# Attention layers of a sparse graph network: queries as two float32r numbers, spread over slots by two products each; slot numbers and owners in 16 bits

## The chip, the core and the metric

The kernel runs on one core of a Trainium2 chip, in one launch. The metric is the device time of that core in microseconds (us). Five engines take part, each with its own queue in program order: TensorE (PE) multiplies matrices into PSUM, VectorE (DVE) and ScalarE (ACT) work element by element, GpSimd (POOL) does some of that and also issues the indirect gathers, and SyncE (SP) issues most other transfers.

## The reference, cut to what matters

Four layers run in a row on x of shape 8 x 2048 x 128, with one sparse 0/1 matrix `adj` (2048 x 2048, symmetric, with its diagonal; about 17 ones in a row). Layers 0 and 2 are masked multi-head attention with a feed-forward part, layers 1 and 3 are graph attention with scores that are sums of two numbers per node.

```
# layers 0 and 2 (8 heads of 16)
Q, K, V = h @ Wq, h @ Wk, h @ Wv
scores  = where(adj == 0, -inf, Q K^T / 4)           # per batch and head
x = layer_norm(h + softmax(scores) V @ Wo + bo)
x = layer_norm(x + relu(x @ W1 + b1) @ W2 + b2)
# layers 1 and 3
h = x @ W;  e = leaky_relu(h @ a_src (of i) + h @ a_dst (of j)), masked by adj
x = layer_norm(softmax(e) h + x)
```

## The kernel before, in words

**Units, steps, slots.** The 2048 nodes are cut into 32 units of 64 nodes (`UNIT`), and the 8 batches into two halves, so that 128 partitions hold 64 nodes of two batch halves. For each unit the kernel lists at run time the neighbours that its nodes need. The list has nine tiles of 128 slots; a slot belongs to one owner node and names one source node. A unit is worked in five steps (`TG`): four of two tiles and a last one of one tile. A dense fallback stands behind a count of rows that don't fit; it is not entered here.

**One step of an attention layer** (`attention`). POOL issues one indirect gather per tile (`gather`, L1671): 128 rows of 8 KB, keys and values of all batches, into one of six `kv` buffers. PE spreads the unit's queries over the step's slots (`spread`, L1734): a 0/1 matrix `hot` (which node owns which slot) times the queries `q_sb`, one product of 32 rows by 512 columns for each tile and batch half, so four of them in a two-tile step, in four different groups of 32 rows of the array; the one-tile step has two of 64 rows. The result `qe` fills four of the eight PSUM banks, and there is one buffer of it. DVE multiplies the gathered keys by `qe` (`multiply`, L1746) and sums over the 16 numbers of a head (`reduce`, L1753). ACT takes the exponential (L1763). POOL, in some steps DVE, multiplies the values by it (`weigh`, L1773; where DVE does it, ACT first writes the exponentials to a PSUM buffer, `ps_e`). PE adds up the slots of each owner with the second half of `hot` (`add`, L1805) into `acc` and `sums`.

**Opening a unit** (`opened`, `fetch`). SP loads the unit's x (L1371, one of four buffers) and its `hot` as 8-bit numbers (L1386); ACT widens `hot` to float32 (L1393, one of three buffers); PE makes the queries in four products of 128 columns (`queries`, L1826, into a PSUM buffer `ps_q`), and ACT copies them out (L1830) into `q_sb`, of which there are two buffers.

**After the last step** (`after_attention`). Division (L1870), transpose (L1482), Wo (L1505), addition (L1882), centring (L1495), norm (L1607, L1640), feed-forward (L1505, L1902, L1912), second norm, store of the new x (L1359), and the projection for the next layer's table (L1535 or L1533, stored at L1593). All these products, the queries, and `ps_e`, share the two PSUM buffers of the pool "m".

**The order.** Nothing is written out in place. Each piece is recorded as an operation with a cost per engine, a key and the cells it reads and writes; a list scheduler (`Plan.order`) walks through assumed time, gives each free engine its ready operation with the lowest key, counts buffers, and so fixes the order on every engine. The engines then run that order with semaphores. The spread has the key of its step minus 6, `queries` and the copy the key of the unit minus 4, most of `after_attention` the key of the unit plus 5. A cost that changes in the code can therefore move any instruction in all queues.

**Graph layers** have the same units and slots. ACT rebuilds the first part of `hot` from the slot numbers (`slot`, L1399) and DVE the second from the owners (`owner`, through `slots`, L1317).

Of the kernel before, what the change touches and what calls it, by code (L numbers as in the profile page):

```python
# [9 lines left out]
F32 = mybir.dt.float32  # L10
# [10 lines left out]
P = 128  # L21
# [747 lines left out]
class Sparse:  # L769
# [15 lines left out]
    def __init__(self, ctx, tc, x, xt, xk, adj, w, out):  # L785
        self.tc, self.nc, self.w, self.xt_in, self.xk_in, self.out = tc, tc.nc, w, xt, xk, out
        self.B, self.N, _ = x.shape
        self.NB = self.N // P
        self.NU = self.N // UNIT
        self.HB = self.B // 2  # L790

        def pool(name, **kw):
            return ctx.enter_context(tc.tile_pool(name=name, **kw))

        self.nc.scalar.preload_act_table_set("natural_log_exp_and_others")
        self.const = pool("const", bufs=1)
        self.dram = pool("dram", bufs=1, space=DRAM)
        self.plan = Plan(self.nc)
        self.op, self.cell = self.plan.op, self.plan.cell
        for tag, bufs in SBUF_BUFS.items():  # L800
            self.plan.pool(tag, pool(f"sb_{tag}", bufs=bufs), bufs, tag in BY_KEY)
        for tag, bufs in PSUM_BUFS.items():
            self.plan.pool(tag, pool(f"ps_{tag}", bufs=bufs, space=PSUM), bufs)

        self.constants()
        self.weights_at = [Cell() for _ in LAYERS]
        self.keys_at = Cell()
        self.late = self.tight = False
        self.whole()
        self.gates = {}  # L810

        self.gate = self.keys_at
        keys = self.const.tile([P, 2 * P], F32, name="Wkv_0")
        self.fill(0, (keys[:, 0:P], w[0]["Wk"]), (keys[:, P : 2 * P], w[0]["Wv"]), at=self.keys_at)
        self.layers = [{"Wkv": keys}]


        self.tables = [
            self.dram.tile([self.N, self.B * (2 * P if kind is MHA else P + 2)], F32, name=f"table_{n}")
            for n, kind in enumerate(LAYERS)  # L820
        ]
        self.table = [Cell() for _ in LAYERS]
        self.rest = [Cell() for _ in LAYERS]

        self.xd = self.dram.tile([self.NU, P, CH], F32, name="xd")
        self.x_at = [Cell() for _ in range(self.NU)]
        self.hots = self.dram.tile([self.NU, P, HOT], F8, name="hots")
        self.hots_at = [Cell() for _ in range(self.NU)]
        self.kept = {}
        self.ends_at = [None] * self.NU  # L830
        self.t = self.const.tile([P, self.NU, P // GROUP * self.HB], F32, name="t")
        self.t_at = [Cell() for _ in range(self.NU)]
        self.idx = self.const.tile([P, self.NU, TILES], I32, name="idx")
        self.idx_at = [Cell() for _ in range(self.NU)]


        self.owner = self.const.tile([P, self.NU, TG, 2], F32, name="owner")
        self.ends = self.const.tile([P, self.NU, 2], F32, name="ends")
        self.late_ends = self.const.tile([P, LATE, 2], F32, name="late_ends")
        self.shift = self.const.tile([P, LATE, 2], F16, name="shift")  # L840

        self.empty = self.const.tile([P, self.NU, TILES], F32, name="empty")


        self.seen = self.const.tile([P, 4, self.NB], F32, name="seen")
        self.stats = self.const.tile([P, 6], F32, name="stats")
        self.eps = self.fixed("eps", EPS)
        self.half = self.fixed("half", 0.5)
        self.rows_n = self.fixed("rows_n", float(self.N))
        self.huge = self.fixed("huge", 1e30)  # L850
# [3 lines left out]
    def constants(self):  # L854
# [5 lines left out]
        self.neg_half = const.tile([P, 4], F32, name="neg_half")  # L860
        nc.gpsimd.memset(self.neg_half, -0.5)

        def ramp(name, shape, pattern, base=0, step=0):
            t = const.tile(shape, F32, name=name)
            nc.gpsimd.iota(
                t, pattern=pattern, base=base, channel_multiplier=step, allow_small_or_imprecise_dtypes=True
            )
            return t


        self.slot = ramp("slot", [P, GS], [[1, GS]])
        for g in range(1, P // GROUP, 2):
            nc.gpsimd.iota(
                self.slot[g * GROUP : (g + 1) * GROUP, GS - P : GS],
# [21 lines left out]
            allow_small_or_imprecise_dtypes=True,  # L896
        )

        self.centre = const.tile([P, P], F32, name="centre")
        nc.vector.tensor_scalar(self.centre, self.ident, -1.0 / P, None, ALU.add)  # L900

# [464 lines left out]
    def fetch(self, n, u, key):  # L1366
# [7 lines left out]
            writes=[x],  # L1374
            dma=P * CH * 4,
        )
        hot = self.cell("hot", [P, HOT])
        if n == 0 and u < KEPT:
            hot8 = self.kept[u]
            self.op({"ACT": 1.05}, lambda e: e.copy(hot.tile, hot8.tile), key - 15, reads=[hot8], writes=[hot])  # L1380
# [312 lines left out]
    def attention(self, n):  # L1693
# [4 lines left out]
        for u, t in self.sequence(0):  # L1698
# [29 lines left out]
            def spread(e, t=t, qe=qe, q=q, hot=hot, tiles=tiles):  # L1728
                for j in range(tiles):
                    for hf in range(2):  # L1730
                        at = (2 * hf + j) * GROUP

                        rows = slice(at, at + GROUP * (3 - tiles))
                        e.matmul(  # L1734
                            qe.tile[:, j, hf, :],
                            lhsT=hot.tile[rows, t * P : (t + 1) * P],
                            rhs=q.tile[rows, :],
                            start=True,
                            stop=True,
                        )  # L1740

            op({"PE": 1.2}, spread, key - 6, reads=[q, hot, *self.sources(n, u, t)], writes=[qe])

            def multiply(e, kv=kv, qe=qe, part=part, tiles=tiles):
                k = part(kv, 0)
# [50 lines left out]
            def add(e, t=t, kv=kv, hot=hot, acc=acc, sums=sums, part=part, exps=exps, tiles=tiles):  # L1796
                weights = exps(kv).rearrange("p (q c) -> p q c", q=2 * tiles)
                for out, rhs in ((acc.tile, part(kv, 1)), (sums.tile, weights)):

                    for j in range(tiles):  # L1800
                        for hf in range(2):
                            at = (2 * hf + j) * GROUP
                            rows = slice(at, at + GROUP * (3 - tiles))
                            col = GS + (2 * t + j) * GROUP
                            e.matmul(  # L1805
                                out[rows, :],
                                lhsT=hot.tile[:, col : col + GROUP * (3 - tiles)],
                                rhs=rhs[:, 2 * j + hf, :],
                                start=(t == 0),
                                stop=(t == TG - 1),  # L1810
                            )
# [5 lines left out]
    def opened(self, n, u, base):  # L1817
# [5 lines left out]
        def queries(e, ps=ps, x=x):  # L1823
            for b in range(hb):
                cols = slice(b * P, (b + 1) * P)
                e.matmul(ps.tile[:, cols], lhsT=x.tile[:, cols], rhs=L["Wq"], start=True, stop=True)  # L1826

        q = cell("q_sb", [P, CH])
        op({"PE": 1.1}, queries, base - 4, reads=[x, self.weights_at[n]], writes=[ps], holds=[q])
        op({"ACT": 0.6}, lambda e, q=q, ps=ps: e.copy(q.tile, ps.tile), base - 4, reads=[ps], writes=[q])  # L1830
        acc = cell("acc", [P, CH])
        sums = cell("sums", [P, hb * H])
        return x, hot, q, acc, sums
# [396 lines left out]
```

## Time and profile before

| | |
|---|---|
| median of 6 runs | 2934.63 us (2930.02 to 2937.98) |
| the profiled execution's own time | 2936.81 us |
| its span in the profile | 2935.0 us |
| mean granted TensorE clock | 0.894 |
| DMA | 1022.52 MB, mean 348 GB/s |
| the list of neighbours and layer 0 | about 0 to 1165 us |
| layer 1 | about 1165 to 1580 us |
| layer 2 | about 1580 to 2500 us |
| layer 3 | about 2490 to 2935 us |

The layers run into each other, so the limits are rough. The profile gives for each engine its busy time and what ended its idle time. A product in float32 is recorded as two pairs of weight load and matmul, so that the four products of a two-tile spread are eight records. Matmul ends are modelled, so a busy PE is not PE at its peak. "Granted clock" is the share of its full speed at which TensorE was clocked.

### The profile page before, as it was taken

What the parts mean: (1) busy time and instruction counts of PE and PEld (TensorE: products, weight loads), DVE (VectorE), ACT (ScalarE), POOL (GpSimd) and SP (SyncE); (2) the same over time, 40 slices, a digit from 0 to 9 for tenths busy, and PEclk for the clock granted to TensorE, in tenths of its full rate; (3) what the DMA queues carried; (4) which work ended last, traced back from release to release, by engine and by line L of the source; (5) the groups of instructions that cost most, each with busy time, mean ns of one, the idle gap of its engine ahead of it and who ended that gap; (6) DMA issues with size and microseconds to landing.
All of it is one profiled execution on the core that took longest, in us unless ns stands there. A gap on an engine that the chain in (4) does not pass through costs nothing.

```text
span 2935.0 us, 59465 instructions
## 1 busy us (share of the span) xinstructions
PE 2277.4 (78%) x21668; PEld 1328.7 (45%) x21668; DVE 2302.2 (78%) x3783; ACT 1419.2 (48%) x4899; POOL 2132.7 (73%) x1456
## 2 busy tenths in 40 slices
PE   6567777778788886888886788888878878777775
PEld 4423333333333434676664343334434333566664
DVE  7789989999889994555554888898898898576665
ACT  5536555555544442655553244444444444354443
POOL 1288877888788855666663877888788786677774
PEclk8779989999899997988987789999999999888887
DMA  8788888899899967999997899999998996999996
GB/s 306 283 323 344 328 324 324 339 353 360 322 345 357 367 262 300 380 405 411 405 407 294 331 353 341 374 364 347 358 383 332 351 380 257 343 409 407 408 395 265
DMA packets 248061, 1022.52 MB, mean 348 GB/s; under 512 B 39184, under 2 KB 52880, under 8 KB 175856
## 3 DMA queue, kind: packets, MB, share of 16 engines
q0 software_dynamic: 166464, 864.44, 75.7%
q1 hardware_dynamic: 81296, 154.18, 14.2%
q8 instruction: 174, 2.85, 0.4%
q14 instruction: 127, 1.04, 0.1%
HBM read 978.23 MB, written 88.08 MB: 363 GB/s over the span
## 4 chain that ended last, share of the span: by engine, by line
DMA 26%; PE 20%; DVE 17%; issue 10%; POOL 7%; ACT 3%; SPq 0%; POOLq 0%; DVEq 0%; ACTq 0%
DMA kv<-table,idx 24%; DVE kv L1746 8%; PE qe L1734 5%; POOL kv L1671 4%; DVE s L1753 4%; POOL kv L1773 3%; PE acc L1805 3%; PE ps_c L1495 2%; DMA hot<-hots 2%; DVE kv L1773 2%; PE ps_y L1912 1%; PE acc_q L2009 1%; PE ps_f L1505 1%; PE ps_t L1482 1%; PE ps_o L1505 1%
## 5 line engine op out<-in xcount | busy, mean ns | idle before, releaser
L1671 POOL DMA_INDIRECT kv<-table,idx x1152 | 1198.2, 1040 | 589.6 <-issue 319.4
L1773 POOL TENSOR_TENSOR kv<-kv 128x2048 f32<-128x2048 f32 x260 | 921.3, 3555 | 72.0 <-ACT kv L1763 67.6
L1746 DVE TENSOR_TENSOR kv<-qe,kv 128x2048 f32<-128x2048 f32 (+1 forms) x320 | 662.1, 2069 | 106.7 <-DMA kv<-table,idx 69.2
L1753 DVE TENSOR_REDUCE s<-kv 128x128 f32<-128x2048 f32 (+1 forms) x320 | 659.6, 2061 | 9.0 <-DVE kv L1746 0.5
L1734 PE MATMUL qe<-q_sb,hot 32*128 32x512 f32 (+1 forms) x2304 | 399.1, 695 | 165.4 <-DVE kv L1746 162.9
L1805 PE MATMUL acc<-kv,hot 128*32 128x512 f32 (+1 forms) x2304 | 369.8, 653 | 56.9 <-POOL kv L1773 26.5
L2009 PE MATMUL acc_q<-kv,w 128*32 128x129 f32 (+1 forms) x4608 | 204.5, 311 | 117.7 <-DVE w L1993 97.4
L1993 DVE TENSOR_TENSOR w<-hot,e 128x512 f32<-128x512 f32 (+1 forms) x384 | 221.3, 597 | 49.4 <-ACT e L1983 34.9
L1763 ACT ACTIVATE kv<-s 128x128 f32<-128x128 f32 (+1 forms) x320 | 95.6, 299 | 319.8 <-DVE s L1753 203.3
L1734 PEld LDWEIGHTS qe<-q_sb,hot 32*128 32x128 f32 (+1 forms) x2304 | 106.9, 196 | 296.3 <-DVE kv L1746 243.0
L2009 PEld LDWEIGHTS acc_q<-kv,w 128*32 128x32 f32 (+1 forms) x4608 | 159.2, 127 | 149.2 <-DVE w L1993 111.1
L1971 DVE TENSOR_TENSOR e<-te,kv 128x16 f32<-128x16 f32 (+1 forms) x320 | 58.5, 183 | 204.8 <-DMA kv<-table,idx 203.3
L1607 ACT ACTIVATE junk<-ps_c 128x128 f32<-128x128 f32 x494 | 136.4, 276 | 158.0 <-PE ps_c L1495 142.2
L1471 ACT COPY trows<-ps_p 128x512 f32<-128x512 f32 (+1 forms) x237 | 112.3, 475 | 189.5 <-PE ps_p L1535 98.0
L1805 PEld LDWEIGHTS sums<-kv,hot 128*32 128x32 f32 (+1 forms) x2304 | 90.4, 119 | 211.7 <-issue 205.7
L1983 ACT ACTIVATE e<-e 128x16 f32<-128x16 f32 (+1 forms) x320 | 65.0, 211 | 240.0 <-DVE e L1978 236.2
L1505 PE MATMUL ps_f<-x,W 128*128 128x512 f32 (+1 forms) x264 | 156.6, 679 | 25.2 <-ACT hidden L1902 17.8
L1495 PE MATMUL ps_c<-centre,r 128*128 128x128 f32 x1024 | 149.8, 293 | 22.2 <-DVE r L1882 11.3
L1495 PEld LDWEIGHTS ps_c<-centre,r 128*128 128x128 f32 x1024 | 129.6, 199 | 65.1 <-DVE r L1882 29.8
L2009 PE MATMUL acc<-kv,w 128*32 128x129 f32 (+1 forms) x2304 | 119.1, 309 | 43.0 <-DVE w L1993 30.6
L1912 PE MATMUL ps_y<-hidden,W 128*128 128x512 f32 (+1 forms) x264 | 142.0, 625 | 8.0 <-ACT hidden L1902 5.5
L1805 PEld LDWEIGHTS acc<-kv,hot 128*32 128x32 f32 (+1 forms) x2304 | 55.8, 115 | 202.5 <-issue 100.6
(204 smaller groups left out, 3878.8 us busy)
## 6 DMA issues: line engine op xcount, KB each, us to landing
x<-xd SPq DMA_DIRECT2D x96, 256.0 KB
xd<-xnew SPq DMA_DIRECT2D x93, 256.0 KB
kv<-table,idx POOLq DMA_INDIRECT x1152
table<-trows SPq DMA_DIRECT2D x128, 130.0 KB
kv<-adj_dram SPq DMA_DIRECT2D x16, 1024.0 KB
table<-trows SPq DMA_DIRECT2D x32, 512.0 KB
table<-trows SPq DMA_DIRECT2D x64, 256.0 KB
kv<-xk_dram SPq DMA_DIRECT2D x8, 1024.0 KB
```

The source lines that it names most:

```text
L1495: e.matmul(ps.tile[:, cols], lhsT=flat(x.tile)[:, cols], rhs=self.centre, start=True, stop=True)
L1505: lambda e: e.matmul(ps.tile, lhsT=w, rhs=x.tile, start=True, stop=True),
L1607: e.activation(self.junk, x, AF.Square, scale=P**-0.5, accum_out=var.tile[:, b, 1:2])
L1671: e.indirect_dma_start(out=rows(kv.tile, j), out_offset=None, in_=self.tables[n][0:nodes], in_offset=bass.IndirectOffsetOnAxis(ap=self.idx ...
L1734: e.matmul(qe.tile[:, j, hf, :], lhsT=hot.tile[rows, t * P : (t + 1) * P], rhs=q.tile[rows, :], start=True, stop=True,)
L1746: e.tensor_tensor(k, qe.tile[:, 0:tiles].rearrange("p j h c -> p (j h) c"), k, ALU.mult)
L1753: e.tensor_reduce(s.tile[:, 0 : tiles * heads].rearrange("p (q c) -> p q c", q=2 * tiles), k, axis=mybir.AxisListType.X, op=ALU.add,)
L1773: e.tensor_tensor(v, v, w.unsqueeze(3).to_broadcast([P, 2 * tiles, heads // 2, HD]), ALU.mult)
L1805: e.matmul(out[rows, :], lhsT=hot.tile[:, col : col + GROUP * (3 - tiles)], rhs=rhs[:, 2 * j + hf, :], start=(t == 0), stop=(t == TG - 1),)
L1912: lambda e, f=f, ps=ps: e.matmul(ps.tile, lhsT=L["W2"][:, f, :], rhs=hidden.tile[:, f, :], start=(f == 0), stop=(f == FFN // P - 1),),
L1993: e.tensor_tensor(w.tile[:, :, j : j + tiles, :].rearrange("p x j c -> p j x c"), oh[:, j : j + tiles].unsqueeze(2).to_broadcast(shape), e ...
L2009: e.matmul(acc(b)[at : at + GROUP * (3 - tiles), :], lhsT=w.tile[:, hf * hb + b, j : j + 3 - tiles, :].rearrange("p j c -> p (j c)"), rhs= ...
```

## The change

- `q_sb` holds two float32r numbers for each query in place of one float32. `queries` now leaves its PSUM group open; ACT copies the product into the first number (as float32r, a 32-bit type of the language); a new product on PE, `less`, adds minus the first number (`minus`, a diagonal of -1) to the same PSUM buffer; ACT copies what is left into the second number.
- `spread` makes, for each tile and batch half, two float32r products that add up in PSUM, one for each number, in place of one float32 product. `hot` of the attention layers is declared float32r, and `add` reads it as float32. The scheduler's cost of a spread goes from 1.2 to 0.8.
- The slot numbers (`slot`) and the owners (`owner`) are kept in float16 in place of float32. They are constants of 1280 and 640 bytes less per partition; `q_sb` takes 4096 bytes more in its two buffers and `minus` 512.

```
-        self.owner = self.const.tile([P, self.NU, TG, 2], F32, name="owner")
+        self.owner = self.const.tile([P, self.NU, TG, 2], F16, name="owner")
...
-        self.slot = ramp("slot", [P, GS], [[1, GS]])
+        self.slot = ramp("slot", [P, GS], [[1, GS]], dtype=F16)
...
+        self.minus = const.tile([P, P], F32R, name="minus")
+        nc.vector.tensor_scalar(self.minus, self.ident, -1.0, None, ALU.mult)
...
-        hot = self.cell("hot", [P, HOT])
+        hot = self.cell("hot", [P, HOT], F32R if LAYERS[n] is MHA else F32)
...
-                        e.matmul(
-                            qe.tile[:, j, hf, :],
-                            lhsT=hot.tile[rows, t * P : (t + 1) * P],
-                            rhs=q.tile[rows, :],
-                            start=True,
-                            stop=True,
-                        )
-
-            op({"PE": 1.2}, spread, key - 6, reads=[q, hot, *self.sources(n, u, t)], writes=[qe])
+                        for k in range(2):
+                            e.matmul(
+                                qe.tile[:, j, hf, :],
+                                lhsT=hot.tile[rows, t * P : (t + 1) * P],
+                                rhs=q.tile[rows, k],
+                                start=k == 0,
+                                stop=k == 1,
+                            )
+
+            op({"PE": 0.8}, spread, key - 6, reads=[q, hot, *self.sources(n, u, t)], writes=[qe])
...
-                                lhsT=hot.tile[:, col : col + GROUP * (3 - tiles)],
+                                lhsT=hot.tile[:, col : col + GROUP * (3 - tiles)].bitcast(F32),
...
-                e.matmul(ps.tile[:, cols], lhsT=x.tile[:, cols], rhs=L["Wq"], start=True, stop=True)
-
-        q = cell("q_sb", [P, CH])
+                e.matmul(
+                    ps.tile[:, cols],
+                    lhsT=x.tile[:, cols],
+                    rhs=L["Wq"],
+                    start=b == 0,
+                    stop=False,
+                    skip_group_check=True,
+                )
+
+        def less(e, ps=ps):
+            e.matmul(
+                ps.tile, lhsT=self.minus, rhs=q.tile[:, 0], start=False, stop=True, skip_group_check=True
+            )
+
+        q = cell("q_sb", [P, 2, CH], F32R)
         op({"PE": 1.1}, queries, base - 4, reads=[x, self.weights_at[n]], writes=[ps], holds=[q])
-        op({"ACT": 0.6}, lambda e, q=q, ps=ps: e.copy(q.tile, ps.tile), base - 4, reads=[ps], writes=[q])
+        op({"ACT": 0.6}, lambda e, q=q, ps=ps: e.copy(q.tile[:, 0], ps.tile), base - 4, reads=[ps], writes=[q])
+        op({"PE": 0.3}, less, base - 4, reads=[q], writes=[ps])
+        op({"ACT": 0.6}, lambda e, q=q, ps=ps: e.copy(q.tile[:, 1], ps.tile), base - 4, reads=[ps], joins=[q])
```

More of the change, by code (lines that the diff above doesn't have):

```diff
@@ L861, in constants, with ramp @@
         nc.gpsimd.memset(self.neg_half, -0.5)
-        def ramp(name, shape, pattern, base=0, step=0):
-            t = const.tile(shape, F32, name=name)
+        def ramp(name, shape, pattern, base=0, step=0, dtype=F32):
+            t = const.tile(shape, dtype, name=name)
             nc.gpsimd.iota(
```

## The prediction

> **What bounds the kernel now.** I read the page's first and fourth part first, then the whole chain by line. The columns are busy time, share of the span and instructions; then shares of the chain that ended last.
>
> ```profile
> PE 2277.4 (78%) x21668; PEld 1328.7 (45%) x21668; DVE 2302.2 (78%) x3783; ACT 1419.2 (48%) x4899; POOL 2132.7 (73%) x1456
> ...
> DMA 26%; PE 20%; DVE 17%; issue 10%; POOL 7%; ACT 3%; SPq 0%; POOLq 0%; DVEq 0%; ACTq 0%
> ```
>
> ```profile
> by line: DMA kv<-table,idx 23.5%; issue 10.3%; DVE kv L1746 7.9%; PE qe L1734 4.7%; POOL kv L1671 4.5%; DVE s L1753 3.6%; POOL kv L1773 3.0%; PE acc L1805 2.8%; PE ps_c L1495 2.0%; DMA hot<-hots 1.6%; DVE kv L1773 1.5%; PE ps_y L1912 1.5%;
> ```
>
> No engine is full and the chain passes through all of them. The spread holds 4.7% of it: 0.047 x 2935 = 138 us. The averages mix four layers, so next come busy times by stretch: the start of layer 2, its steady part, and the steady part of layer 0.
>
> ```profile
> core 0: us, PE busy (x) PEld busy (x) DVE busy (x) ACT busy (x) POOL busy (x), PEclk, DMA share, GB/s
> 1580.00:1800.00 220.00, 165.75 (x1047) 74.48 (x1048) 172.79 (x126) 75.27 (x251) 163.93 (x97) 0.82 0.89 341
> 1880.00:2480.00 600.00, 494.57 (x3502) 230.71 (x3494) 526.95 (x398) 282.06 (x964) 487.31 (x273) 0.98 0.92 355
> 450.00:1060.00 610.00, 494.51 (x3478) 233.89 (x3476) 549.95 (x545) 312.02 (x1055) 516.32 (x282) 0.94 0.91 346
> ```
>
> In steady attention DVE is busy 88 to 90%, PE 81 to 82%, POOL 81 to 85% (without the 0.30 us between two gathers), the DMA engines 91 to 92%: four resources near their limit, held up by each other's queues. So I asked what DVE waits for in layer 2 (1600 to 2490 us); columns are total us, times, longest.
>
> ```profile
> DVE kv L1773 <- ACT ps_e L1763: 33.2, 8, 6.0
> DVE r L1882 <- PE ps_o L1505: 25.9, 9, 5.6
> DVE kv L1746 <- PE qe L1734: 19.7, 12, 5.3
> DVE kv L1746 <- DMA kv<-table,idx: 11.5, 12, 2.7
> ```
>
> DVE is idle there for some 107 us; about half ends with a PE product, and the largest single row with an exponential that stood behind the copy of late queries. Gathers end little of it.
>
> **The spread, before and after.** Its records, and those of products of other widths and types:
>
> ```profile
> 2129.16 1.14 PE L1734 MATMUL qe<-q_sb,hot 32*128 32x512 f32 x8 [1.30 <-DVE kv L1746]
> ...
> L1734 PE MATMUL qe<-q_sb,hot x2304: 587/692/1219, 132.3 to 2483.8; 32*128 32x512 f32 x192
> ...
> L1495 PE MATMUL ps_c<-centre,r x1024: 272/275/582, 190.9 to 2525.6; 128*128 128x128 f32 x171
> ...
> L1248 PE MATMUL ps_l<-unit_aux,hot x160: 198/204/280, 48.9 to 775.5; 128*128 128x86 f16 x160
> L1188 PE MATMUL ps_aux<-aux,to_unit x32: 182/182/219, 35.2 to 724.0; 128*128 128x45 f16 x28, 128*128 128x48 f16 x4
> ```
>
> From 128 to 512 columns a float32 record grows by (587 - 272)/384 = 0.82 ns a column, with 0.17 us fixed. From 45 to 86 columns a float16 record grows by (198 - 182)/41 = 0.39 ns, or by 0.54 with the medians: about half. Eight records of 0.59 us or more end within 1.14 us, so the four groups of rows run side by side: weights 0.11, first round 0.43, second round 0.43, tail 0.17. The change has again eight records, two for each group, with the same weights twice. If float32r streams as float16 does (the nearest row, and one record per product where float32 has two), each round is about 0.22 us: 0.11 + 0.22 + 0.22 + 0.17 = 0.72 us. It saves 0.43 us, 38%, in each of 320 steps, or 137 us of PE. No float32r record is in this trace: the bounds are no saving (each round stays at 0.43), and this.
>
> What of it lies on the path? The reduce (2.27 us) runs on DVE beside the next spread, which can start as soon as the multiply has freed the one `qe`; there a shorter spread is worth nothing. But PE's queue is in order: while the spread runs, the adds that free `kv` buffers and the products of the unit before stand behind it. The chain weighs both: 138 us of the 399.1 us that the spread is busy. I take 38% of 138 = 52 us; the low end is the direct waits alone (29.4 us in 22 visits over the span: 22 x 0.43 = 9 us). **-52.**
>
> **`less` and the second copy.** One product of 128 rows by 512 columns, one round: 0.11 + 0.22 + 0.17 = 0.50 us, 64 times, 32 us of PE. PE's chain share is 0.20 x 2935 = 587 us of 2277 busy, 26%: **+8** (0 to 32). One more copy of 128x512 on ACT (before: 64 of median 0.585 us) is 37 us; ACT's chain share is 88 of 1419 us, 6%: **+2** (0 to 37); what hides it is ACT's 52% of idle time.
>
> **Opening a unit later.** The queries are whole only after copy, `less` and copy: 0.50 + 0.59 + two hand-overs of about 0.05 = 1.2 us more, and `ps_q` keeps one of the two "m" buffers that much longer, at least. Behind it wait the first spread of the unit and all products that need an "m" buffer. The order of the built program shows where this can bite: `less` stands behind the last spread of the unit before in 10 units of layer 0 and 7 of layer 2; 17 x 1.2 = 20 us at most. In these places the spread must also wait for the multiply of the one-tile step (1.22 us), which covers nearly all of it: **+5** (0 to 20; if that cover is gone in all 64 units, 77).
>
> **The order moves.** Costs feed the scheduler, so all queues are rearranged. Before, the queries as a whole stand behind the last spread of the unit before in 8 units of layer 2 (every third or fourth), and the chain of late work there ends in the 33.2 us of the table above. After, they do so in none; and SP issues the load of `hot` straight behind that of x in 20 units of layer 2, where it was 5, with fewer loads behind the store of the new x (5, where 12), which waits for the norm. Part of this gain is in the 52 us already: **-10** (0 to -33).
>
> **The clock.** PE gets lighter, and that has a price. Columns as in the stretches above:
>
> ```profile
> 2086.98:2090.40 3.42, 1.30 (x13) 0.52 (x5) 2.88 (x2) 1.73 (x3) 3.42 (x1) 0.99 1.03 394
> 2090.40:2093.81 3.41, 3.41 (x4) 1.34 (x5) 0.00 (x0) 1.22 (x3) 2.92 (x4) 0.51 0.98 374
> ```
>
> A stretch with PE busy for 1.30 of 3.42 us is followed by one at half clock, in which DVE does nothing at all. Layer 2's start, with PE busy 75%, was granted 0.82. Taking 0.43 us out of each step makes more such stretches. If both steady parts fell to the 0.89 of the whole span, their 495 + 495 us of PE would grow by 10% and 6%, 78 us, of which 26% on the path: 20 us. I take half: **+10** (0 to 20).
>
> The page "TensorE: Matmul & The Clock Gate" of the Trainium skill (section "Why this matters for your kernels") speaks against lighter PE work in its way: gaps between bursts of more than about 3 us bring the half clock back. By that rule 0.43 us less work would add no such gap, and the sum would be 10 us lower; the stretch above was not a gap and still lost the clock, so here the measurement decides.
>
> **Nothing.** Slot numbers in float16: ACT's row from `slot` takes 0.828 us at the median whether it writes float16 (L1224) or float32 (L1399). Owners: the row on DVE takes 0.484 us for float32 output and 0.477 for float16. 96 and 64 times 0.01 us stay under 2 us either way. Widening `hot` to float32r and the bitcast in `add` change no size; `minus` is one short operation at the start.
>
> **Sum.** -52 + 8 + 2 + 5 - 10 + 10 = -37. The profiled execution's own time is 2936.8 us (span 2935.0), 2.2 above the median of the runs: 2936.8 - 37 - 2.2 = **2898 us**. Best ends together (-52 - 33 + 8 + 2) give 2860.
>
> **Rivals.** *Slower: the spread was covered (chance 0.17).* For it speaks the 2.27 us reduce beside a 1.14 us spread and only 29.4 us of direct waits; against it the chain's 138 us. Then -9 + 8 + 2 + 5 + 10, and nothing from the order: +16, 2951 us. It decides where less than half of the 52 us comes back, since the new work, the opening and the clock cost 25. *The change doesn't do what it says (0.07).* If a float32r round takes as long as now, the costs remain: 2960. If the eight products don't run side by side, a spread takes 0.11 + 8 x 0.22 + 0.17 = 2.04 us, 0.9 more; 320 times, 35% on the chain: +100, near 3060. Against it: float32 pairs do run side by side today. *No difference (0.09).* POOL and the gathers take over: in the 600 us POOL is busy 487 and waits another 79 in front of gathers, mostly for its own issuing, so little more than 5% is free; if most of the gain ends there, 2929 to 2940.
>
> **Chances.** Faster 0.67 (from the forecast and, with a lucky order, down to 2855), same 0.09, slower 0.17 + 0.07 = 0.24. 0.2%, 6 us, is about what a measurement of this kernel can tell from no change. The range 2855 to 2957 takes in the best ends and the covered spread, and leaves out the second part of the 0.07 and tails.
>
> **What would show it.** Right: the 512-column records of the spread fall from 587/692 to about 390 ns and an x8 group from 1.14 to near 0.7 us; PE's busy time falls by some 100 us; the spread's chain share falls well below 4.7%; the waits for `ps_e` and `ps_o` in layer 2 shrink; the granted clock drops a little; layers 1 and 3 keep their length. Wrong: the x8 group stays above 1 us; or it shrinks and DVE's idle time in 1600 to 2490 only changes its name, to `q_sb`, POOL or gathers.

## The result, and the profile after

The changed kernel takes **2955.96 us** (median of 20 runs, 2945.69 to 2966.12), the kernel before 2934.44 (46 runs, 2920.58 to 2942.85): the ratio is 1.0076, interval 1.0065 to 1.0086. It is 22 us slower, where 37 us faster was forecast, and lies just inside the range. The profiled execution has a span of 2956.7 us, its granted clock is 0.866 on the mean (0.894 before). The last two runs told below (the second number made by VectorE, the fast spread in the order of 0.8) were taken while every kernel run then, the one before included (3156.34 us), took 7% longer, with transfers in layer 1 at 334 to 339 GB/s where the profile of before has 386, so they are read by ratio and by their attention layers alone.

The spread itself did what was forecast. The first fence has the records of the spread and of the new `less` in the changed kernel (L1737 and L1839; smallest, middle and largest duration in ns), and one spread of a two-tile step from its timeline.

```profile
L1737 PE MATMUL qe<-q_sb,hot x2304: 382/492/793, 134.5 to 2487.8; 32*128 32x512 f32 x192
L1839 PE MATMUL ps_q<-q_sb,minus x64: 474/503/1415, 133.0 to 2454.1; 128*128 128x512 f32 x64
659.78 0.75 PE L1737 MATMUL qe<-q_sb,hot 32*128 32x512 f32 x8 [1.84 <-DVE kv L1749]
```

The float32 records were 587/692/1219 and a group of eight took 1.14 us; now it takes 0.75 (forecast: 0.72). The spread's busy time fell from 399.1 to 267.1 us. But the page's first part and the three stretches of the forecast say what became of these 132 us (columns: length; busy us and instructions of PE, weight loads, DVE, ACT, POOL; granted clock; DMA share; GB/s).

```profile
PE 2221.4 (75%) x21732; PEld 1370.1 (46%) x21732; DVE 2313.0 (78%) x3789; ACT 1448.4 (49%) x4957; POOL 2140.1 (72%) x1457
```

```profile
core 0: us, PE busy (x) PEld busy (x) DVE busy (x) ACT busy (x) POOL busy (x), PEclk, DMA share, GB/s
1580.00:1800.00 220.00, 154.84 (x1097) 77.80 (x1099) 177.23 (x135) 82.31 (x265) 164.14 (x95) 0.83 0.89 337
1880.00:2480.00 600.00, 476.88 (x3493) 247.03 (x3493) 531.89 (x392) 290.46 (x984) 490.18 (x274) 0.92 0.93 355
450.00:1060.00 610.00, 478.11 (x3422) 245.99 (x3423) 538.29 (x550) 319.18 (x1058) 502.17 (x277) 0.89 0.90 343
```

PE as a whole fell by 56 us only. `less` takes 38 us of the difference (64 records of 590 ns on the mean). The rest is that the other products, added up by line, take 48 us more than before (lines overlap, so this does not add up exactly): the granted clock in the steady part of layer 2 went from 0.98 to 0.92, in layer 0 from 0.94 to 0.89. The next fence has what DVE waits for in layer 2 (1600 to 2490 us; total us, times, longest).

```profile
DVE kv L1749 <- DMA kv<-table,idx: 63.9, 38, 8.7
DVE kv L1749 <- PE qe L1737: 13.0, 14, 2.0
...
DVE kv L1776 <- ACT ps_e L1766: 3.6, 5, 1.8
DVE r L1899 <- PE ps_o L1507: 2.0, 3, 1.1
```

The waits for `ps_e` and `ps_o`, 33.2 and 25.9 us before, are nearly gone, as forecast. The wait for gathers, 11.5 us before, is now 63.9. All idle time of DVE in this stretch went from 113.5 to 105.5 us only: for the most part one wait took the other's name, which the forecast had given as a sign of being wrong.

By the first `multiply` of each unit, the changed kernel is 15 us late at unit 31 of layer 0, 9 late at the start of layer 2, level at its last unit, and 22 late at the end of the program: layer 2 gained some 10 us up to its last unit, that unit lost 4, and the step to layer 3 and that layer lost 18.

### The profile page after: what moved, and what is told of

It is laid out like the page before. It is cut to its first block, busy times and chain, and to the rows that moved or that the text cites. A ratio compares the mean times of both kernels' runs of the same rounds, so it can differ in the third digit from the quotient of the medians.

```text
span 2956.7 us, 59637 instructions
## 1 busy us (share of the span) xinstructions
PE 2221.4 (75%) x21732; PEld 1370.1 (46%) x21732; DVE 2313.0 (78%) x3789; ACT 1448.4 (49%) x4957; POOL 2140.1 (72%) x1457
## 5 line engine op out<-in xcount | busy, mean ns | idle before, releaser
L1808 PE MATMUL acc<-kv,hot 128*32 128x512 f32 (+1 forms) x2304 | 391.6, 688 | 65.3 <-POOL kv L1776 51.8
L1737 PE MATMUL qe<-q_sb,hot 32*128 32x512 f32 (+1 forms) x2304 | 267.1, 491 | 207.0 <-DVE kv L1749 202.2
L1737 PEld LDWEIGHTS qe<-q_sb,hot 32*128 32x128 f32 (+1 forms) x2304 | 111.6, 205 | 334.2 <-DVE kv L1749 256.8
L2026 PEld LDWEIGHTS acc_q<-kv,w 128*32 128x32 f32 (+1 forms) x4608 | 160.2, 128 | 155.6 <-DVE w L2010 113.5
L1473 ACT COPY trows<-ps_p 128x258 f32<-128x258 f32 (+1 forms) x238 | 112.8, 475 | 167.8 <-PE ps_p L1537 90.8
L1919 ACT ACTIVATE hidden<-ps_f,b 128x512 f32<-128x512 f32 (+1 forms) x126 | 85.4, 678 | 130.0 <-PE ps_f L1507 127.4
L1484 PE MATMUL ps_t<-ident,normed 128*128 128x128 f32 x638 | 122.5, 321 | 31.0 <-ACT normed L1642 10.7
```

Of the source, the lines that this page charges most:

```text
L1484: e.transpose(ps.tile[:, b * P : (b + 1) * P], flat(x.tile)[:, b * P : (b + 1) * P], self.ident)
L1737: e.matmul(qe.tile[:, j, hf, :], lhsT=hot.tile[rows, t * P : (t + 1) * P], rhs=q.tile[rows, k], start=k == 0, stop=k == 1,)
L1808: e.matmul(out[rows, :], lhsT=hot.tile[:, col : col + GROUP * (3 - tiles)].bitcast(F32), rhs=rhs[:, 2 * j + hf, :], start=(t == 0), stop=( ...
L2026: e.matmul(acc(b)[at : at + GROUP * (3 - tiles), :], lhsT=w.tile[:, hf * hb + b, j : j + 3 - tiles, :].rearrange("p j c -> p (j c)"), rhs= ...
```

## The experiments

All runs are compared with the kernel before on the same chip, by ratio; one us is 0.034%. "Order" is the order of all queues. Four theories stood at the start: the new **order** lost the time; the lower **clock** ate the gain; the spread was **covered** by other work; the **opening** of a unit (copy, `less`, copy) cost more than forecast.

### The parts alone, in the old order

Order alone: one number of the kernel before.

```
-            op({"PE": 1.2}, spread, key - 6, ...
+            op({"PE": 0.8}, spread, key - 6, ...
```

> The kernel before with one number changed: the plan's cost of a spread is 0.8 instead of 1.2 us. The products stay float32, there is no `less` and no second copy; only the order of the queues differs. Theory 1 (the new order lost the time): 2945 to 2960 us, most of the 21 us that the change lost. Theory 2 (a lighter TensorE is granted a lower clock) and theory 3 (the spread was covered, gathers take over): as before, 2930 to 2940, with the clock at 0.89. Theory 4 (the opening of a unit, `less` and the second copy): as before, 2930 to 2940.

Fast spread alone, in the old order (`q` and `hot` are float32r; the cut is shortened):

```
+                        for k in range(2):
                             e.matmul(qe..., lhsT=hot..., rhs=q.tile[rows, :], start=k == 0, stop=k == 1)
             op({"PE": 1.2}, spread, key - 6, ...
```

> The kernel before with each spread made of two one-pass float32r products, both of the queries' first number (so the queries come out rounded and doubled; the second number, `less` and the second copy are left out). The plan's cost stays 1.2, so all queues stand exactly as before: only the spread's length changes. Theory 1 (order) and theory 4 (opening): the 52 us of the forecast come back when order and opening are left alone, 2880 to 2905. Theory 2 (clock): the granted clock in the steady part of layer 2 falls from 0.98 to about 0.91 and eats more than half, 2915 to 2940. Theory 3 (covered): the waits for gathers in layer 2 grow from 11.5 to over 50 us and the time stays at 2925 to 2935, at whatever clock.

Opening alone, issued in the place of the one copy (shortened):

```
+        def copies(e, q=q, ps=ps):
+            e.copy(q.tile[:, 0], ps.tile)
+            self.nc.tensor.matmul(ps.tile, lhsT=self.minus, rhs=q.tile[:, 0], start=False, stop=True, ...)
+            e.copy(q.tile[:, 1], ps.tile)
```

> The kernel before with the queries made into two float32r numbers by copy, `less` and second copy, put into the queues at the very place of the one copy, so that all else stands as before; slot numbers and owners in 16 bits to make room. The spread stays one float32 product each, of the first number alone (the second is computed and not used). Theory 4 (opening): 2960 to 2980, since the change's loss and what the spread gives back both sit here. Theories 1, 2 and 3: 2937 to 2952, the +15 us that the forecast gave to `less`, the second copy and the later opening, or less.

Both together, still in the old order:

> The whole change, with the queues in the order of before (plan's cost 1.2; copy, `less` and second copy stand where the one copy stood). Theory 1 (order): the gain is there without the new order, 2890 to 2915, over 40 us under the changed kernel. Theory 2 (clock): 2935 to 2955, with the clock at about 0.87 as in the changed kernel. Theory 3 (covered): 2935 to 2950, the opening's cost on a spread that gives nothing. Theory 4 (opening): 2945 to 2960, about the changed kernel's time, and about 20 us less than the opening alone.

| run | median us | before | ratio | interval | difference, us |
|---|---|---|---|---|---|
| order alone (0.8) | 2952.89 | 2941.37 | 1.0040 | 1.0022 to 1.0057 | +12 |
| fast spread alone | 2929.15 | 2941.37 | 0.9965 | 0.9951 to 0.9978 | -10 |
| opening alone | 2967.19 | 2941.37 | 1.0089 | 1.0066 to 1.0112 | +26 |
| fast spread and opening | 2952.14 | 2941.37 | 1.0044 | 1.0023 to 1.0065 | +13 |

The parts add up: -10 + 26 = +16 against +13 measured, and with the order's +12 some +28 against the +22 of the changed kernel, within the intervals. The second sum is weaker than it looks. The order of the changed kernel is not that of the order alone (`less` and the second copy are operations of their own in it), and two other orders of the same parts, below, cost +65 and +21; that +28 comes near +22 may be partly luck. No theory takes all. The opening is the largest term, the order costs where it was to gain, and the spread gives a fifth of its forecast.

The order alone, 2953 us, lies in the band of its theory. The fast spread alone, at 2929 us, lies in the bands of two theories, clock (2915 to 2940) and covered (2925 to 2935), and the sign of neither came: the granted clock from 1880 to 2480 us is 0.96, where 0.91 was expected, and DVE's wait for gathers in layer 2 is 13.0 us, where over 50 were. The whole change in the old order lies in the bands of clock and opening; the opening alone, 2967 us, speaks for the opening.

**Where the spread's gain went.** The page of the fast spread alone, which has the order of before: its first part, the two largest PE groups, and then the chain by line.

```profile
PE 2190.4 (75%) x21668; PEld 1355.8 (46%) x21668; DVE 2303.7 (79%) x3783; ACT 1419.8 (49%) x4899; POOL 2133.8 (73%) x1456
...
L1806 PE MATMUL acc<-kv,hot 128*32 128x512 f32 (+1 forms) x2304 | 385.4, 679 | 87.9 <-POOL kv L1774 51.9
L1735 PE MATMUL qe<-q_sb,hot 32*128 32x512 f32 (+1 forms) x2304 | 260.5, 479 | 187.8 <-DVE kv L1747 186.4
```

```profile
by line: DMA kv<-table,idx 21.5%; issue 11.8%; DVE kv L1747 7.6%; POOL kv L1671 4.9%; POOL kv L1774 4.9%; DVE s L1754 3.6%; PE acc L1806 3.0%; PE acc_q L2010 2.2%; PE qe L1735 1.9%; PE ps_c L1495 1.8%; PE ps_f L1505 1.3%; PE ps_te L2033 1.3
```

The spread is 139 us shorter, PE as a whole 87. The products that nobody touched, added up by line, take 2061 us on PE where they took 2012: at the lower clock (0.876 for 0.894) 49 us came back, a good third. The `add` is the largest of them, 385.4 us for 369.8, and it now waits 51.9 us for POOL's `weigh` where it waited 26.5. In the chain the spread fell from 4.7% (138 us) to 1.9% (55), and POOL's `weigh` rose from 3.0% to 4.9%, "issue" from 10.3% to 11.8%, together 97 us more. The chain let the spread go and took other work in its place. What did fall is DVE's direct wait for the spread over the whole span, here before, with the fast spread, and in the two filled kernels of the next part (filled before, fast spread filled):

```profile
DVE kv L1746 <- PE qe L1734: 29.4, 22, 5.3
```

```profile
DVE kv L1747 <- PE qe L1735: 19.8, 19, 3.3
```

```profile
DVE kv L1746 <- PE qe L1734: 49.3, 40, 3.7
```

```profile
DVE kv L1747 <- PE qe L1735: 31.4, 22, 4.9
```

It fell by 9.6 us, and the time by 10; in the filled pair by 17.9, and the time by 18. With one round it fell by 11.3 us for a gain of 9. With the opening in place it fell by 6.5, for a gain of 13. These are single profiles, but the size is near that of the gain each time, and far under the 52 us that the chain gave.

### How much one us of each engine is worth

A still shorter spread, one float32r product (`for k in range(1)`), and the fast spread with TensorE filled up again, and the filling alone (shortened):

```
+                if t < TG - 1:
+                    for k in range(2):
+                        e.matmul(sums.tile[:, CH // 2 : CH], lhsT=hot.tile[:, 0:P], rhs=hot.tile[:, 0 : CH // 2],
+                                 start=False, stop=False, skip_group_check=True)
             op({"PE": 1.5}, add, ...
```

> The kernel before with each spread made of one single one-pass float32r product (the queries' first number once; the second number, `less` and the second copy are left out), all queues as before. A spread of eight should take about 0.5 us where the two-round one takes 0.75 and float32 1.14. Covered (the wait only changes its name): no more than a few us beyond the two rounds' gain of 10, 2920 to 2930. Spread on the path and eaten by the clock: the granted clock falls under 0.87 and the time stays or turns, 2925 to 2945. Spread on the path at 26 to 38%: another 20 to 30 us, 2895 to 2910.

> The run with the fast spread in the old order, and TensorE given back the work that it saved: behind the products of each two-tile `add`, two float32 products of 256 columns (0.43 us) into unused columns of the sums' bank. The output is that of the fast spread with its doubled queries. Clock theory: the granted clock comes back to 0.89 or more, and with it the time that the clock ate: 2895 to 2915. Covered: the clock comes back and the time does not, 2925 to 2935. If the length of TensorE's queue is what counts, whoever fills it: about before, 2935 to 2945.

> The kernel before with the same filling behind the products of each two-tile `add`: TensorE gets 0.43 us more work in 256 steps, 110 us in all, and nothing else changes. Clock theory: a higher granted clock (over 0.90) pays for part of it, 2925 to 2945. Covered (TensorE has slack of this size and the clock matters little): 2940 to 2955. If TensorE's queue sits on the path with 26 to 38% of its work: 2970 to 2985.

A quarter less work in each `reduce` (DVE) and in each `weigh` (POOL):

```
-                    k,
+                    k[:, :, :, 0 : HD - HD // 4],
...
+                d = HD if e is self.nc.vector else HD - HD // 4
+                v = v[:, :, :, 0:d]
```

> The kernel before with a quarter less work in each `reduce` (12 of the 16 products of each head are summed, the other four left out): 0.57 us less on VectorE in 256 steps and half of it in 64, some 165 us in all; all queues as before. It asks what stands behind the saved TensorE time. If VectorE covers the spread (its steps follow one another and TensorE fits beside them): at least half comes back, 2830 to 2860. If the gathers and GpSimd's issuing of them do: 2915 to 2935, as with the shorter spread. If all four resources hold one another: a fifth to a third, 2885 to 2905.

> The kernel before with a quarter less work in each `weigh` on GpSimd (12 of 16 values of each head are weighed, the other four left as they are): some 230 us less on GpSimd, all queues as before. If GpSimd and the gathers behind it are what takes over when the spread gets short: 2820 to 2880. If VectorE is: 2915 to 2935. If all hold one another: 2870 to 2900.

| run | ratio (interval) | time, us | busy time of the engine, us | us of time per us of engine | clock |
|---|---|---|---|---|---|
| one round | 0.9968 (0.9950 to 0.9985) | -9 | PE -117 | 0.08 | 0.851 |
| fast spread (above) | 0.9965 | -10 | PE -87 | 0.12 | 0.876 |
| fast spread, filled | 1.0016 (0.9999 to 1.0033) | +5 | PE +88 | 0.05 | 0.903 |
| before, filled | 1.0079 (1.0061 to 1.0098) | +23 | PE +176 | 0.13 | 0.917 |
| fast spread, filled, against before, filled | 1.0016 against 1.0079 | -18 | PE -88 | 0.21 | 0.903 against 0.917 |
| short `reduce` | 0.9904 (0.9883 to 0.9925) | -28 | DVE -144 | 0.20 | 0.890 |
| short `weigh` | 0.9909 (0.9889 to 0.9929) | -27 | POOL -214 | 0.13 | 0.901 |

The first part of the page of the two filled kernels (fast spread, then before) and of the two with less work elsewhere (`reduce`, then `weigh`) gives the busy times of this table:

```profile
PE 2364.9 (80%) x22692; PEld 1518.3 (52%) x22692; DVE 2305.7 (78%) x3783; ACT 1417.8 (48%) x4899; POOL 2138.1 (73%) x1456
```

```profile
PE 2452.9 (83%) x22692; PEld 1500.8 (51%) x22692; DVE 2304.6 (78%) x3783; ACT 1419.6 (48%) x4899; POOL 2133.2 (72%) x1456
```

```profile
PE 2279.3 (78%) x21668; PEld 1338.6 (46%) x21668; DVE 2158.7 (74%) x3783; ACT 1416.7 (49%) x4899; POOL 2132.4 (73%) x1456
```

```profile
PE 2255.7 (78%) x21668; PEld 1323.3 (46%) x21668; DVE 2301.5 (79%) x3783; ACT 1419.5 (49%) x4899; POOL 1919.2 (66%) x1456
```

The filling came out larger than its expectation said: in the kernel before its products are busy for 298.6 us (1.17 a step, not 0.43), while at the higher clock the rest of PE got 72 us shorter, added up by line. So the filling does not just give back what the spread had saved, and the bands of its two expectations don't apply. The third row is no price: a shorter spread and a longer filling are both in it, and its interval takes in 1.0. The two filled kernels against each other are the clean pair.

Three readings follow. PE's time is worth 0.08 to 0.21 us each, in both directions, and not the 0.38 of the forecast. The clock can have kept back a part of the gain only: with PE filled and the clock above 0.9 in both kernels the fast spread is worth 18 us instead of 10 (a fuller PE may be a reason too), and the 52 of the forecast stay far off. And no other engine is the one behind it: a us of DVE is worth 0.20, of POOL 0.13, so a shorter step on one engine runs into the next of them. Both times, 2909 and 2910 us, fell between the expected bands, a little above those for four resources that hold one another (up to 2905 and 2900). With the short `reduce`, DVE waits in layer 2 34.4 us for the spread (19.7 before) and 31.6 for gathers (11.5). One round, 2929 us, lies in the bands of both covered and clock.

### The opening of a unit

Two copies without `less`, and a second number made by VectorE (shortened):

```
-            self.nc.tensor.matmul(ps.tile, lhsT=self.minus, ...)
-            e.copy(q.tile[:, 1], ps.tile)
+            self.nc.vector.tensor_tensor(q.tile[:, 1], ps.tile, q.tile[:, 0].bitcast(F32), ALU.subtract)
```

> The run of the opening alone without its `less` and without the sum that stays open for it: the queries are copied twice from the same product, all else stands as before, the spread is float32 and reads the first copy. It splits the 26 us of the opening. If the second copy on ScalarE is the price: 2955 to 2967. If the round trip over TensorE is (ScalarE stands still until `less` has come through TensorE's queue): 2937 to 2945, since a copy alone was costed at 2 us.

> The whole change in the old order (cost 1.2), with the second number made in another way: VectorE subtracts the first number from the sum in PSUM and writes the rest, so that there is no `less` on TensorE and no second copy on ScalarE, which goes on behind its one copy. The output keeps both numbers. If the round trip through TensorE's queue is the opening's price: 2930 to 2943, the short spread's -10 and 47 us of VectorE (64 of some 0.74 us) at the 16% that its time is worth by the short reduce, and a little for its own wait. If any second number costs the 26 us: 2948 to 2956, as with the whole change in the old order.

Two copies took 2940.58 us against 2938.62, ratio 1.0023 (1.0003 to 1.0044): 7 us by the ratio, in the band for the round trip, so `less` and the wait for it are the other 19 of the 26. The next three fences are waits before the second number: ACT's second copy in the run of the opening alone, DVE's subtraction, and the two copies of the changed kernel.

```profile
ACT q_sb L1844 <- PE ps_q L1841: 59.1, 64, 6.6
```

```profile
DVE q_sb L1841 <- ACT q_sb L1840: 47.9, 23, 7.9
```

```profile
ACT q_sb L1845 <- PE ps_q L1829: 37.7, 32, 5.2
ACT q_sb L1847 <- PE ps_q L1839: 30.1, 33, 5.0
```

In the run of the opening alone ACT stands still in all 64 openings, up to 6.6 us, until `less` has come through PE's queue; in the changed kernel in 33. What then comes next on ACT is an exponential in 20 of the 64 openings, and in the others work of the norms, the feed-forward, the tables or the list of neighbours. DVE's wait for `ps_e` over the span grew from 39.2 to 47.3 us, POOL's for its exponentials not at all (67.6 and 67.7). PE pays too: it stands in front of `less` for the first copy, and then for the second copy, which frees the "m" buffer:

```profile
PE ps_q L1841 <- ACT q_sb L1840: 13.8, 24, 1.6
PE ps_t L1484 <- ACT q_sb L1844: 13.1, 22, 0.7
```

Before, the transposes (`ps_t`) waited 4.0 us for the one copy. How the 19 us split over these waits is not shown. The subtraction, with no round trip over PE, was no cheaper: 3183.66 us against 3156.34, ratio 1.0090 (1.0063 to 1.0117), with the fast spread in it. Its attention layers say the same: units 4 to 31 and 34 to 63 take 827 and 826 us, where the whole change in the old order has 814 and 822 and the fast spread alone 802 and 804. There DVE stands 47.9 us behind ACT's first copy and works 43.8 us more, and PE's transposes wait 24.0 us for the subtraction. So the cost is not TensorE's part as such: in both forms that were run, the engine that makes the second number stands still for another engine at the opening of a unit.

### The order

The changed kernel with cost 1.2, the kernel before with 1.0:

> The changed kernel with the plan's cost of a spread put back to 1.2 us; `less` and the second copy stay operations of the plan. If the number 0.8 made the bad order: 2940 to 2950, the fixed-order sum of opening and spread (+13) or a little better, since ScalarE's stall is shorter in the changed kernel. If any new order costs about 10 us, whatever the number: 2950 to 2962. In this program the products for the last but one table store of layer 2 stand 1.5 spreads before the end of the layer (5 in the kernel before, half a spread in the changed one), which speaks for the second.

> The kernel before with the plan's cost of a spread at 1.0, half way to the changed kernel's 0.8, and nothing else. If the time follows the number: about 2944, half of the 12 us that 0.8 costs. If each number is a draw of its own: anywhere in 2930 to 2960; by the place of the products for the last but one table store (1.5 spreads before the end of layer 2, where it is 5) the step to layer 3 should come late again, 2945 to 2958.

3002.44 us (1.0220, 1.0199 to 1.0241), far above both of its bands, and 2939.46 (1.0016, 0.9999 to 1.0032). In the kernel before the time may follow the number, +5 at 1.0 and +12 at 0.8; in the changed kernel it does not, since its own 0.8 is better than 1.2 by 1.4%. By the first `multiply` of each unit and against the kernel before, most of the loss at 1.2 comes between units 16 and 31 of layer 0 (30 us), between unit 34 and the end of layer 2 (23) and behind it (13); why is open.

The run of the order alone shows what the new order does in layer 2 without any faster product; DVE's waits from 1600 to 2490 us:

```profile
DVE kv L1746 <- DMA kv<-table,idx: 53.4, 42, 4.6
...
DVE kv L1773 <- ACT ps_e L1763: 5.4, 5, 3.6
...
DVE r L1882 <- PE ps_o L1505: 3.5, 5, 2.1
```

The 59.1 us of waits for `ps_e` and `ps_o` shrink to 8.9, and those for gathers grow from 11.5 to 53.4. All idle time of DVE in this stretch is about the same, 112.5 us by 113.5. The wait that the forecast counted as a gain was exchanged for another. From unit 34 to 63 this order takes 820.1 us (815.9 in the run with the earlier store below, which has the same queues up to unit 61), before 811.5. A further 15 us are lost between the last `multiply` of layer 2 and the end; the changed kernel loses 18 there, the whole change in the old order 6. Its place looks plain in the timeline of the order alone: the third table store from the end of layer 2, and POOL's first gather of layer 3 (2487.69 and 2491.66 before).

```profile
2506.89 1.09 SPq L1593 DMA_DIRECT2D table<-trows  x2
...
2510.76 1.03 POOL L1671 DMA_INDIRECT kv<-table,idx  x1 [27.95 <-issue]
```

Two kernels move that store forward, by one due time (orders of 0.8 and 1.0):

```
-        key = base + TG
+        key = base + TG - (5 if n == 2 and self.NU - 3 <= u < self.NU - 1 else 0)
```

> The kernel before with the plan's cost of a spread at 0.8, as in the run of the order alone, and one more number: in layer 2 the work behind the attention of the two units before the last gets a due time 5 steps earlier. The products for the third table store from the end move from behind 319.4 to behind 317.2 of the 320 adds, where the kernel before has them; nothing before unit 61 moves. If the order's loss sits at the step from layer 2 to layer 3: it goes, 2934 to 2942. If it is spread over the layers: 2947 to 2955, as with the order alone.

> The kernel before with cost 1.0 and the same earlier due time. In the order of 1.0 layer 2 ended 22 us earlier than in the kernel before, and 17 of them were lost again at the step to layer 3. If that step is the place: 2918 to 2927. If not: 2936 to 2943.

```profile
2498.77 1.09 SPq L1593 DMA_DIRECT2D table<-trows  x2
...
2502.65 1.02 POOL L1671 DMA_INDIRECT kv<-table,idx  x1 [13.15 <-PE ps_te L2032]
```

In the trace (order 0.8) the store came 8 us earlier and the loss behind layer 2 shrank from 14.6 to 2.8 us. The times say otherwise: 2945.88 us, ratio 1.0041 (1.0022 to 1.0061), as without it. For 1.0: 2934.80, ratio 0.9992 (0.9974 to 1.0010), 7 us under the run without it, with intervals that overlap, and with the median 1 us below the band for another place and 8 above the band for this step. One profiled execution and medians that scatter by 20 us don't agree here; how much of the order's loss sits at that step stays open.

### Do the terms hold in other orders

> One float32r product for each spread (second number, `less` and second copy left out, as in the run of one round), cost 1.0 and the earlier due time. If the terms add up: the 10 us of the short spread on top of the order's 12 to 16, 2906 to 2917. If the short spread's gain belongs to the old order: 2918 to 2930.

> The changed kernel with cost 1.0 and the earlier due time; both numbers of the queries, `less` and second copy as it has them. If the terms add up: 16 us of opening and spread on top of an order worth -14, 2930 to 2942, at least 14 us under the changed kernel. If the opening's price hangs on where the plan puts `less`: anything up to the 3002 us that cost 1.2 gave.

> The kernel before with the plan's cost 0.8 and each spread made of two one-pass products of the first number (the second number, `less` and the second copy are left out, the queries come out doubled): the order of the first run, with the fast spread. If the terms add up over orders: 2941 to 2947 (+12 and -10), and the opening then costs some 20 us in the changed kernel's order. If the short spread is worth nothing there: 2948 to 2955.

One round with cost 1.0 and the earlier due time: 2920.57 us, ratio **0.9948** (0.9929 to 0.9967). This lies in the band for a gain that belongs to the old order, but the bands took that order to be worth -12 to -16 us, and by itself it measured -2; with the terms as measured, -2 and -9, the sum is -11 for -15 found, within the intervals. It beats both kernels, by 15 and some 37 us; it keeps one float32r number of the queries and leaves out the second. The whole change in that order: 2956.18 us, ratio 1.0073 (1.0045 to 1.0100), no better than the changed kernel. The expected 2930 to 2942 leant on a profile of cost 1.0 that was 8 us under its own median; but from the measured -2 too the sum is only about +11, and +21 was found (13 to 29). So opening and order do not simply add up, and the 3002 us of cost 1.2, +65 for the same parts, say so more strongly. The fast spread in the order of 0.8: 3142.35 us against 3156.34, ratio 0.9959 (0.9943 to 0.9975). It can't be added to the order's +12 from another set. From unit 34 to 63 it takes 812.4 us where that order took 820.1 and 815.9, from unit 4 to 31 804 where it took 805 and 806; in the old order 811.5 went to 804.1 and 806 to 802. So the short spread's gain is not tied to the old order, though its size elsewhere is less sure.

## Why the prediction was wrong, step by step

**The spread, -52: measured -10.** The duration was right (0.75 us for 0.72). The step that failed is "the chain weighs both": 38% of the spread's 138 us in the chain was taken as gain. The share of a step in the chain says that it was the last to end in that execution, not by how much. The low end of the forecast, the direct waits alone (-9), was the right size: with the fast spread they fell by 9.6 us, and the time by 10. The rival "spread was covered" had this mechanism; it forecast 2951 us, 5 under the result, with nothing for the order and 11 too little for the opening, so that its number is partly luck. Of the 59 us between forecast and result, the spread with the clock is 32, the order 22 and the opening 11, as measured one by one (65 together).

**The clock, +10: inside the -10 above.** The fall of the granted clock was forecast and came. With it 49 of 139 us came back; at 0.12 us per us of PE that is worth about 6 us, an estimate, and the filled pair, worth 18 where the spread alone is 10, does not contradict it. The time at half clock from 1880 to 2480 us, counted in the clock's records, was 27 us before, 52 with the fast spread, 130 with one round, 101 after, and 20 with PE filled. The page "TensorE: Matmul & The Clock Gate" of the Trainium skill (section "Why this matters for your kernels") names idle gaps over about 3 us as what brings half clock; in the same 600 us each of the five profiles has 3 or 4 gaps of more than 3 us between matmuls, so here they do not decide, and the measurement does.

**`less`, second copy and opening, +15: measured +26, in the fixed order.** The copy was 7 by the ratio (forecast 2). Too small were the other two, +13 together for 19: their price was taken from PE's chain share and from the places where `less` stands behind the last spread, and the standstill of ACT in front of the second copy was put at nothing beyond `less` itself. It was 59 us in the fixed order and 30 in the changed kernel. Which of the waits behind it make up the price stays open.

**The order, -10: measured +12.** Here the sign was wrong. That queries stand behind the last spread was read well, and that wait did vanish. What would come in its place, the gathers, was in the rival "no difference" with 5% left to POOL; it was not applied to this term.

**Nothing, 0.** 16-bit slot numbers and owners were not measured alone; they are in the runs of the opening, also in that of two copies, which cost 7 us in all.

Right beside these: the record times, the fall of the granted clock, the waits for `ps_e` and `ps_o`, layer 1 unchanged. PE's busy time was to fall by some 100 us and fell by 56. Layer 3 was to keep its length; with the step before it, it lost 18 us.

## What to carry to other kernels

Where four resources are each 80 to 90% busy and hold one another up, price a saving on one of them by the direct waits for it, or by a run that lengthens that step; the share in the chain of work that ended last overstates it, here by a factor of five. A second step on the way from a product to its user can cost far more than its own duration where an engine with an ordered queue must wait for it: here the second copy cost 7 us, with `less` in between 26. When a scheduler's cost changes with the code, test the new order alone before anything else: here one number alone moved the time by 0.4% in the kernel before and by 1.4% in the changed one.

## What the hardware showed that was not expected

- Half clock follows lightly busy stretches, not only gaps. In layer 0 of the kernel before (440 to 1150 us), cut into the stretches of 3.41 us in which the clock is granted, all 12 full-clock stretches with PE busy under 40% are followed by one at half clock, 8 of 13 with 40 to 50%, and 2 of 154 above that. Adding 299 us of useless products raised the mean clock from 0.894 to 0.917 and cost only 23 us.
- One float32r round instead of two takes 0.50 us instead of 0.75 for a two-tile step, but the clock fell to 0.851, and of the 80 us that the spread got shorter only 30 show in PE's busy time.
